# A graph convolution with a two-expert feed-forward layer: the order of the prelude, and where the first node tile's counts, its sums and one check stand

## The chip, the cores and the metric

The kernel runs on one core of a Trainium2 chip. The core has five engines, each with its own instruction queue worked off in order: PE (TensorE, matmuls; PEld are its weight loads), DVE (VectorE), ACT (ScalarE), POOL (GpSimd) and SP (SyncE, which here only issues DMAs). They wait for each other through semaphores. The metric is the device time of one execution in microseconds (us). Three runs of the kernel before gave 1189.58, 1190.65 and 1191.01 us; the median is 1190.65.

## The reference

6250 nodes with 256 features and 206250 edges (100000 drawn ones in both directions, and one loop per node), sorted by destination. First a graph convolution with a residual, then a feed-forward layer of eight experts with a residual, of which the two best of one common routing are used for all nodes:

```python
deg = segment_sum(ones, dst) + 1                  # a second loop per node is added
dinv = rsqrt(deg)
h = layernorm(x) @ W
out = segment_sum(h[src] * (dinv[src] * dinv[dst])[:, None], dst) + b
x = x + where(out > 0, out, prelu_a * out)
...
y = einsum(gelu(einsum(x, W1) + b1), W2) + b2     # per expert
x = x + layernorm(sum of the top-2 experts' y * weight + x) * gamma + beta
```

## The kernel before

Nodes are cut into 49 tiles of 128 (`NT`). For the first 41 node tiles (`NDT`) the neighbour sums are dense: a matrix of edge counts of one destination tile against all 49 source tiles is built from one-hot vectors (`one_hots` on DVE, `counts` on PE, a copy `a_t` by ACT in `counts`), and is multiplied with the scaled h (`sums` on PE, 49 matmuls of 128x512 per node tile; h is held in two parts, high and low, side by side, hence 512). For the last 8 tiles (`NGT`) rows of h are gathered by indirect DMA and summed by one-hot matmuls (`g_hot`, `g_sums`, `fetch`).

Everything up to that is the prelude, and the change is there. Its order is written out by hand: inside `manual_schedule` every engine gets its instructions in program order, so the order of the calls is the order of each queue.

- `x_load(i)` (L223) loads seven node tiles of x by SP. `h_step(m)` (L354) transposes two node tiles of x on PE (`pt`, L361), copies them by ACT (`xT`, L365), multiplies the pair of the step before with the centred weight on PE (`p`, L372) and copies that to `hk` by ACT (L376). There are 26 steps; `h_some(n)` (L380) runs the next n. `p` has two buffers (`ps_h`).
- `x_stats(i)` (L389) takes the statistics of seven node tiles on DVE (L391); from them `rs`, 1/sqrt of the variance, is made (L515 to L523).
- `search(w)` (L406) finds, on ACT and DVE, where the edges of 5 node groups begin (w = 0 to 4), and POOL gathers their packed edges from memory (`run`, L427, five indirect DMAs; three buffers). `keys(w)` (L437, DVE) makes keys of them, `turn_keys(w)` (L445) transposes keys and low parts on PE and copies them by ACT to `keyT` and `loT` (L457), `key_hots(w)` (L462, DVE) derives from `keyT` what the degrees are counted from (`ev`).
- Then the degrees: 49 thin matmuls (L529), `deg` on DVE (L535), a square root on ACT (L536), its reciprocal on DVE (L545), and `sc` = `rs` x `dinv` (L546).
- `least` is the least key, for a check of the edge list; `less` (L538 to L544) halves `keyT` by minima down to 400 elements before the reduction at L554. `pto`, `tto` (L548 to L552) are sums over the degrees from which `g_at` (L582) is made, the place of the gathered tiles' edges.
- `parts(n)` (L558) scales node tile n of h by `sc`: the high part on ACT (L565), the low one on DVE (L571), or, for every fifth tile after the first 14, on ACT and POOL (L568, L569).
- The main part (from L587) opens with the remaining `parts`, in between which the counts of tile 0 are placed (L798 to L808). `keep(i)` (L785) writes seven finished node tiles to memory by SP, for the gathers. `g_edges()` (L701) gathers on POOL the edges of the last 8 tiles.
- The loop (L812) handles node tile n in four quarters: one-hots of the next tile, counts of tile n + 1 (L817), a quarter of the sums of n (L819), and the tile before is finished (`node`, `stat`). `own(n)` adds the extra loop of each node. After tile `G0` - 2 = 2 `g_check()` (L709) puts the checks together, with a matmul on PE in its middle (L724); the result decides later on whether a slow fallback runs.

Buffers that matter: `hk` is in two halves (`h_room(0)`, `h_room(1)`, 24 node tiles each, `HK` = 24) that lie where the count matrices of even and odd tiles come later (tags a0 and a1), so counts of tile 0 can be stored only when the parts of tiles 0 to 23 have been read. `one_hots` has two pairs of buffers, the count results in PSUM (`pa`) four.

Of the kernel before, what the change touches and what calls it, by code (L numbers as in the profile page):

```python
# [11 lines left out]
F32 = mybir.dt.float32  # L12
BF16 = mybir.dt.bfloat16
# [21 lines left out]
def gnn_moe_kernel(  # L35
# [147 lines left out]
    with ExitStack() as ph:  # L183
# [196 lines left out]
        def h_some(n):  # L380

            for m in itertools.islice(steps, n):
                h_step(m)
                n -= 1
            return n == 0
# [3 lines left out]
        def x_stats(i):  # L389
            for t in range(TB):  # L390
                nc.vector.bn_stats(st[:, i * TB + t, :], xbs[i][:, t, :])  # L391
# [79 lines left out]
        for i in range(2, NB_T):  # L471
            x_load(i)
        for _ in range(3):
            h_some(2)
            search(_)
            if _ > 0:
                x_stats(_ - 1)
        h_some(2)
        search(3)
        keys(0)  # L480
        h_room(1)
        hk.append((2 * HK, 1, hk2))
        h_some(1)
        turn_keys(0)
        x_stats(2)
        h_some(1)
        key_hots(0)
        search(4)
        h_some(1)
        keys(1)  # L490
        h_some(1)
        turn_keys(1)
        x_stats(3)
        h_some(1)
        key_hots(1)
        h_some(1)
        keys(2)
        turn_keys(2)
        x_stats(4)
        h_some(1)  # L500
        key_hots(2)
        h_some(2)
        keys(3)
        turn_keys(3)
        x_stats(5)
        h_some(1)
        key_hots(3)
        h_some(2)
        keys(4)
        turn_keys(4)  # L510
        x_stats(6)

        dm = ep.tile([P, NT], F32, name="dm")
        va = ep.tile([P, NT], F32, name="va")
        nc.vector.tensor_tensor(dm, st[:, :, 1], st[:, :, 4], OP.subtract)  # L515
        nc.vector.tensor_tensor(va, st[:, :, 2], st[:, :, 5], OP.add)
        nc.vector.scalar_tensor_tensor(dm, dm, 0.25, dm, op0=OP.mult, op1=OP.mult)
        nc.vector.scalar_tensor_tensor(va, va, 1.0 / D, dm, op0=OP.mult, op1=OP.add)
        nc.vector.tensor_scalar(va, va, LN_EPS, None, op0=OP.add)
        nc.scalar.activation(rs, va, AF.Sqrt)  # L520
        h_some(1)
        key_hots(4)
        nc.vector.reciprocal(rs, rs)  # L523
        h_some(1)

# [10 lines left out]
        nc.scalar.activation(dinv, deg, AF.Sqrt)  # L536
        nc.vector.tensor_reduce(tot[:, 0:1], deg, AX.X, OP.add)
        less = rp_.tile([P, WP, P, 2], F32, name="run")  # L538
        less = less.rearrange("p j e f -> p (j e f)").bitcast(BF16)
        halves, m = keyT, NPR  # L540
        while m > 400:
            m //= 2
            nc.vector.tensor_tensor(less[:, :m], halves[:, :m], halves[:, m : 2 * m], OP.min)
            halves = less  # L544
        nc.vector.reciprocal(dinv, dinv)  # L545
        nc.vector.tensor_tensor(sc, rs, dinv, OP.mult)  # L546

        pto = ps_h.tile([P, 2, D], F32, name="p")  # L548
        nc.tensor.matmul(pto[:NT, 0, :P], deg, ones, start=True, stop=True)
        tto = ep.tile([P, P], F32, name="tto")  # L550
        nc.scalar.copy(tto[:NT], pto[:NT, 0, :P])
        nc.tensor.matmul(pto[:, 1, :NGT], tto[:NT], g_before[:NT], start=True, stop=True)  # L552
        least = ep.tile([P, 1], F32, name="least")
        nc.vector.tensor_reduce(least, less[:, :m], AX.X, OP.min)  # L554
        nc.vector.tensor_scalar(tot[:, 1:2], least, 0.0, None, op0=OP.is_lt)


# [18 lines left out]
        while h_some(1):  # L576
            for n in itertools.islice(ns, 2):
                parts(n)
        g_s = ep.tile([P, NGT], F32, name="g_s")
        nc.vector.tensor_tensor(g_s, pto[:, 1, :NGT], g_first, OP.subtract)  # L580
        nc.vector.tensor_scalar(g_s, g_s, 0.0, float(E - GE), op0=OP.max, op1=OP.min)
        nc.vector.tensor_scalar(g_at, g_s, g_part, None, op0=OP.add)  # L582
        nc.vector.tensor_reduce(tot[:, 3:4], deg[:, NDT:], AX.X, OP.add)
        for n in itertools.islice(ns, 4):
            parts(n)

    with main:  # L587
# [121 lines left out]
        def g_check():  # L709
# [3 lines left out]
                op0=OP.mult, op1=OP.add,  # L713
            )
            some = gp.tile([P, 2 * D], F32R, name="rows").bitcast(F32)[:, : NGT * GC]
            flat = g_neg.rearrange("p g c -> p (g c)")
# [73 lines left out]

        kept = 0
        for n in ns:
            parts(n)
            if n % TB == TB - 1:
                for kept in range(kept, n // TB + 1):
                    keep(kept)
                kept += 1
            if n == HK - 6:  # L798
                one_hots(0)
                one_hots(1)  # L800
            if n in (HK + 6, NT - 1):
                c = 0 if n < NT - 1 else 2
                for b in range(NBH):
                    counts(0, c * NBH + b)
                one_hots(c + 2)
                for b in range(NBH):
                    counts(0, (c + 1) * NBH + b)
                one_hots(c + 3) if c == 0 else None  # L808
        g_edges()

        assert NHG == QT
        for n in range(NDT):  # L812
            for c in range(NHG):
# [456 lines left out]
```

## Time and profile before

The page describes one execution of 1190.92 us; the span from its first to its last instruction is 1189.1 us. The mean granted clock of TensorE was 0.962.

| engine | busy us | share of the span |
|---|---|---|
| PE | 1100.9 | 93% |
| PEld | 842.6 | 71% |
| DVE | 711.5 | 60% |
| ACT | 630.9 | 53% |
| POOL | 529.1 | 44% |

The share is a mean over stages. By windows of the timeline, with the busy us of each engine in it:

| stretch, us | PE | DVE | ACT | POOL | granted clock |
|---|---|---|---|---|---|
| 0 to 20 | 11.95 | 14.03 | 3.85 | 7.99 | 1.00 |
| 20 to 40 | 14.32 | 10.81 | 12.63 | 10.97 | 0.93 |
| 40 to 60 | 19.05 | 16.91 | 13.75 | 15.55 | 0.89 |
| 60 to 80 | 18.17 | 13.63 | 12.52 | 0.95 | 0.96 |
| 80 to 100 | 9.62 | 12.71 | 15.44 | 4.02 | 0.76 |
| 100 to 120 | 6.11 | 20.00 | 16.56 | 10.35 | 0.50 |
| 120 to 140 | 20.00 | 11.33 | 8.49 | 15.73 | 0.93 |
| 140 to 160 | 20.00 | 16.13 | 9.68 | 4.38 | 1.00 |

The first four rows are the edges, the steps of h and the keys; the degrees are at 75 to 80 us, the parts from 82 to 117, and the loop over node tiles runs from about 119 to 790 us. Behind it come the routing and the feed-forward stage, up to 1189. The granted clock is the share of TensorE's full speed that the throttle gave; at 0.50 a matmul takes about twice as long. In lines of the timeline the columns are: start, duration, engine, line, operation, what is written and read, the shapes, how often, and in brackets the idle time of the engine before it with what ended it.

### The profile page before, as it was taken

To read this page: it belongs to the slowest core of one execution; us is meant where nothing else is said; L and a number is where in the kernel's file an instruction comes from. 1 tells how busy PE (TensorE), PEld (TensorE's weight loads), DVE (VectorE), ACT (ScalarE), POOL (GpSimd) and SP (SyncE) were. 2 spreads that over 40 slices of the span, in tenths; PEclk is the share of its full clock that TensorE was granted. 3 is DMA by queue.
4 is the path that set the end of the run, shared out by engine and by line. 5 is a ranking of instruction groups with operands and counts; after the bars stand their busy time and mean duration, and the time that the engine had idled before them with its cause. 6 is when DMAs were issued, how large, how long until landed. Compare 5 with 4: busy or idle time off the path is not lost. (4 is left out here: it accounts for less than half of the span.)

```text
span 1189.1 us, 18227 instructions
## 1 busy us (share of the span) xinstructions
PE 1100.9 (93%) x6706; PEld 842.6 (71%) x6706; DVE 711.5 (60%) x1509; ACT 630.9 (53%) x1547; POOL 529.1 (44%) x526
## 2 busy tenths in 40 slices
PE   7882999999999999999999999952999999999996
PEld 5671878888888888888888888841666666666665
DVE  6759677788787887878878788653222232222222
ACT  3658446666666666666666666611333333333332
POOL 3704703555565555655556555400333333334433
PEclk9895999999999999999999999985999999999998
DMA  8708603565655656556565565504011111111000
GB/s 266 227 12 323 187 27 98 143 155 147 153 141 143 156 146 154 138 143 157 146 154 138 144 157 144 133 23 135 14 42 49 37 36 36 36 36 36 23 18 22
DMA packets 92254, 133.11 MB, mean 112 GB/s; under 512 B 8830, under 2 KB 47390, under 8 KB 92158
## 3 DMA queue, kind: packets, MB, share of 16 engines
q0 software_dynamic: 43584, 80.40, 27.6%
q1 hardware_dynamic: 45266, 49.06, 12.6%
q10 hardware_dynamic: 3308, 2.41, 0.7%
q8 instruction: 54, 0.88, 0.3%
q14 instruction: 42, 0.34, 0.1%
HBM read 104.47 MB, written 27.37 MB: 111 GB/s over the span
## 5 line engine op out<-in xcount | busy, mean ns | idle before, releaser
L659 PE MATMUL po<-hp,a_t 128*128 128x512 f32 x2009 | 504.2, 400 | 0.0
L745 POOL DMA_INDIRECT rows<-hl_d,g_src x288 | 329.2, 1143 | 299.1 <-PE pg L776 228.5
L659 PEld LDWEIGHTS po<-hp,a_t 128*128 128x128 f32 x2009 | 367.1, 189 | 72.7
L643 ACT CAST a_t<-pa 128x392 fp32r<-128x392 f32 x656 | 271.0, 501 | 206.2 <-PE pa L639 204.5
L605 DVE TENSOR_TENSOR oh_lo<-iota,loT 128x2048 bf16<-128x2048 bf16 x164 | 199.5, 1216 | 15.9 <-PE pa L639 15.9
L639 PEld LDWEIGHTS <-oh_lo 128*128 128x128 bf16 x2624 | 128.5, 99 | 68.2 <-issue 25.4
L1200 PE MATMUL p<-xT,w_sb 128*128 128x512 f32 (+1 forms) x416 | 172.6, 573 | 2.5 <-ACT hT L1204 1.8
L639 PE MATMUL pa<-oh_key,oh_lo 128*128 128x98 bf16 x2624 | 153.6, 211 | 22.9 <-DVE oh_key L605 12.3
L1218 PE MATMUL p<-w_sb,hT 128*128 128x256 f32 (+1 forms) x784 | 172.9, 381 | 0.0
L1218 PEld LDWEIGHTS p<-w_sb,hT 128*128 128x128 f32 (+1 forms) x784 | 148.5, 191 | 20.2
L605 DVE TENSOR_TENSOR oh_key<-iota,keyT 128x1568 bf16<-128x1568 bf16 x164 | 158.2, 965 | 0.0
L1200 PEld LDWEIGHTS p<-xT,w_sb 128*128 128x128 f32 x416 | 77.6, 192 | 90.9 <-issue 86.4
L1223 DVE TENSOR_TENSOR yt<-yt,p 128x256 f32<-128x256 f32 (+1 forms) x49 | 20.6, 421 | 164.3 <-PE p L1218 164.3
L1184 POOL TENSOR_TENSOR yt<-yt,b_sb 128x1024 f32<-128x1024 f32 (+1 forms) x13 | 29.1, 2242 | 184.0 <-PE px L1178 124.6
L1204 ACT ACTIVATE hT<-p,b_sb 128x512 f32<-128x512 f32 (+1 forms) x104 | 67.5, 661 | 79.0 <-PE p L1200 78.7
L759 ACT ACTIVATE oh_g<-iota_f,g_dst 128x128 fp32r<-128x128 f32 x288 | 103.8, 425 | 0.0
L776 PE MATMUL pg<-rows,oh_g 128*128 128x512 f32 x288 | 91.1, 397 | 0.0
L1228 ACT ACTIVATE rs<-rs 128x1 f32<-128x1 f32 (+1 forms) x49 | 9.9, 203 | 146.4 <-DVE rs L1227 146.4
L674 DVE TENSOR_TENSOR x<-x,po 128x256 f32<-128x256 f32 x41 | 17.3, 422 | 104.9 <-ACT x L673 104.9
L1233 POOL TENSOR_TENSOR yt<-yt,gamma_bc 128x256 f32<-128x256 f32 (+1 forms) x49 | 35.5, 725 | 90.2 <-DVE yt L1230 90.2
L760 ACT ACTIVATE oh_g<-oh_g 128x256 fp32r<-128x256 f32 x144 | 60.3, 419 | 4.5
L1173 DVE TENSOR_SCALAR yt<-xt,mean,rstd 128x256 f32<-128x256 f32 x49 | 18.8, 444 | 73.0 <-DMA xt<-x_d 72.8
(195 smaller groups left out, 863.3 us busy)
## 6 DMA issues: line engine op xcount, KB each, us to landing
hl_d<-hp SPq DMA_DIRECT2D x7, 1792.0 KB, 10.9
x_d<-x SPq DMA_DIRECT2D x49, 128.0 KB, 1.7
xt<-x_d SPq DMA_DIRECT2D x12, 512.0 KB, 3.9
out_dram<-yt SPq DMA_DIRECT2D x48, 128.0 KB, 1.7
xb<-in_x_dram SPq DMA_DIRECT2D x6, 896.0 KB, 11.9
xs<-in_x_dram SPq DMA_DIRECT2D x41, 128.0 KB, 3.4
rows<-hl_d,g_src POOLq DMA_INDIRECT x288, 3.8
w_sb<-in_L_ffn_W_dram ACTq DMA_DIRECT2D x2, 512.0 KB, 7.8
```

The costliest lines, as they stand in the source:

```text
L605: nc.vector.tensor_tensor(oh, iota2[:, :m, :].unsqueeze(1).to_broadcast([P, HG // 2, m, 2]), v[:, s].rearrange("p (q t) -> p q t", t=2).un ...
L639: nc.tensor.matmul(pa[:, i].rearrange("p j h -> p (j h)"), oh_lo[:, q, :, t], oh_key[:, q, :, t], start=True, stop=True,)
L643: nc.scalar.copy(tiles[n][:, :, b * 2 * BG : (b + 1) * 2 * BG], pa.rearrange("p i j h -> p h (i j)"),)
L659: nc.tensor.matmul(pouts[n].rearrange("p k d -> p (k d)"), tiles[n][:, g, :], hp2[g // TB][:, g % TB].rearrange("p k d -> p (k d)"), start ...
L745: nc.gpsimd.indirect_dma_start(out=g_rows[j], out_offset=None, in_=hl_d, in_offset=bass.IndirectOffsetOnAxis(ap=g_src[:, j // GC, j % GC : ...
L759: nc.scalar.activation(oh[:, i, :], iota_f, AF.Abs, bias=g_neg[:, g, c : c + 1])
L760: nc.scalar.activation(oh, oh.bitcast(F32), AF.Relu, scale=-1.0, bias=1.0)
L776: nc.tensor.matmul(pouts[n].rearrange("p k d -> p (k d)"), oh[:, i, :], g_rows.pop(j0 + i), start=False, stop=((j0 + i) % GC == GC - 1),)
L1200: nc.tensor.matmul(p1[:, :cols], w1_sb[:, e, k, f * P : (f + 1) * P], xT[:, k, :cols], start=(k == 0), stop=(k == ND - 1),)
L1204: nc.scalar.activation(hT[:, e, f, :cols], p1[:, :cols], AF.Gelu, bias=b1_sb[:, e, f : f + 1])
L1218: nc.tensor.matmul(p2[:r], hT[:, e, f, t * P : t * P + r], w2_sb[:, e, f, :], start=(e == 0 and f == 0), stop=(e == TOP_K - 1 and f == NF ...
L1233: nc.gpsimd.tensor_tensor(y, y, gamma_bc[:r], OP.mult)
```

## The change

The h steps are spread in another way: twelve of the 26 come ahead of the first `keys`, then two or three between one turn of keys and its hots, one in the last round, and none between the last hots and the degrees; three are left for the loop with the parts. The statistics follow the keys by three batches. `search(4)` comes ahead of the first keys. The halvings of `less` go; the least key is taken by one reduction over all 3200 elements of `keyT`, in `g_check`. `pto`, `tto` and the sum of the degrees come behind the last steps of h. The first one-hots of tile 0 come directly behind the prelude, its counts at parts 23, 27 and 31, its sums from part 32 on, each behind the part that it uses; the one-hots of tile 1 begin at parts 38 and 44, its counts follow the last part. The loop then begins at tile 1.

```diff
@@ -470,58 +470,40 @@
 
         for i in range(2, NB_T):
             x_load(i)
-        for _ in range(3):
-            h_some(2)
-            search(_)
-            if _ > 0:
-                x_stats(_ - 1)
+        h_some(2)
+        search(0)
+        h_some(2)
+        search(1)
+        x_stats(0)
+        h_some(2)
+        search(2)
+        x_stats(1)
         h_some(2)
         search(3)
-        keys(0)
+        h_some(1)
+        search(4)
+        x_stats(2)
         h_room(1)
         hk.append((2 * HK, 1, hk2))
-        h_some(1)
-        turn_keys(0)
-        x_stats(2)
-        h_some(1)
-        key_hots(0)
-        search(4)
-        h_some(1)
-        keys(1)
-        h_some(1)
-        turn_keys(1)
-        x_stats(3)
-        h_some(1)
-        key_hots(1)
-        h_some(1)
-        keys(2)
-        turn_keys(2)
-        x_stats(4)
-        h_some(1)
-        key_hots(2)
-        h_some(2)
-        keys(3)
-        turn_keys(3)
-        x_stats(5)
-        h_some(1)
-        key_hots(3)
-        h_some(2)
-        keys(4)
-        turn_keys(4)
-        x_stats(6)
+        h_some(3)
 
         dm = ep.tile([P, NT], F32, name="dm")
         va = ep.tile([P, NT], F32, name="va")
-        nc.vector.tensor_tensor(dm, st[:, :, 1], st[:, :, 4], OP.subtract)
-        nc.vector.tensor_tensor(va, st[:, :, 2], st[:, :, 5], OP.add)
-        nc.vector.scalar_tensor_tensor(dm, dm, 0.25, dm, op0=OP.mult, op1=OP.mult)
-        nc.vector.scalar_tensor_tensor(va, va, 1.0 / D, dm, op0=OP.mult, op1=OP.add)
-        nc.vector.tensor_scalar(va, va, LN_EPS, None, op0=OP.add)
-        nc.scalar.activation(rs, va, AF.Sqrt)
-        h_some(1)
-        key_hots(4)
+        for w in range(NW):
+            keys(w)
+            turn_keys(w)
+            if w + 3 < NB_T:
+                x_stats(w + 3)
+            if w + 4 == NB_T:
+                nc.vector.tensor_tensor(dm, st[:, :, 1], st[:, :, 4], OP.subtract)
+                nc.vector.tensor_tensor(va, st[:, :, 2], st[:, :, 5], OP.add)
+                nc.vector.scalar_tensor_tensor(dm, dm, 0.25, dm, op0=OP.mult, op1=OP.mult)
+                nc.vector.scalar_tensor_tensor(va, va, 1.0 / D, dm, op0=OP.mult, op1=OP.add)
+                nc.vector.tensor_scalar(va, va, LN_EPS, None, op0=OP.add)
+                nc.scalar.activation(rs, va, AF.Sqrt)
+            h_some(1 if w == NW - 1 else 2 + w % 2)
+            key_hots(w)
         nc.vector.reciprocal(rs, rs)
-        h_some(1)
 
 
         pdeg = pcnt[:, NW : NW + NT]
@@ -534,26 +516,8 @@
         deg = ep.tile([P, NT], F32, name="deg")
         nc.vector.tensor_scalar(deg, pdeg, 1.0, None, op0=OP.add)
         nc.scalar.activation(dinv, deg, AF.Sqrt)
-        nc.vector.tensor_reduce(tot[:, 0:1], deg, AX.X, OP.add)
-        less = rp_.tile([P, WP, P, 2], F32, name="run")
-        less = less.rearrange("p j e f -> p (j e f)").bitcast(BF16)
-        halves, m = keyT, NPR
-        while m > 400:
-            m //= 2
-            nc.vector.tensor_tensor(less[:, :m], halves[:, :m], halves[:, m : 2 * m], OP.min)
-            halves = less
         nc.vector.reciprocal(dinv, dinv)
         nc.vector.tensor_tensor(sc, rs, dinv, OP.mult)
-
-        pto = ps_h.tile([P, 2, D], F32, name="p")
-        nc.tensor.matmul(pto[:NT, 0, :P], deg, ones, start=True, stop=True)
-        tto = ep.tile([P, P], F32, name="tto")
-        nc.scalar.copy(tto[:NT], pto[:NT, 0, :P])
-        nc.tensor.matmul(pto[:, 1, :NGT], tto[:NT], g_before[:NT], start=True, stop=True)
-        least = ep.tile([P, 1], F32, name="least")
-        nc.vector.tensor_reduce(least, less[:, :m], AX.X, OP.min)
-        nc.vector.tensor_scalar(tot[:, 1:2], least, 0.0, None, op0=OP.is_lt)
-
 
         def parts(n):
             i, t = divmod(n, TB)
@@ -576,13 +540,18 @@
         while h_some(1):
             for n in itertools.islice(ns, 2):
                 parts(n)
+
+        pto = ps_h.tile([P, 2, D], F32, name="p")
+        nc.tensor.matmul(pto[:NT, 0, :P], deg, ones, start=True, stop=True)
+        tto = ep.tile([P, P], F32, name="tto")
+        nc.scalar.copy(tto[:NT], pto[:NT, 0, :P])
+        nc.tensor.matmul(pto[:, 1, :NGT], tto[:NT], g_before[:NT], start=True, stop=True)
         g_s = ep.tile([P, NGT], F32, name="g_s")
         nc.vector.tensor_tensor(g_s, pto[:, 1, :NGT], g_first, OP.subtract)
         nc.vector.tensor_scalar(g_s, g_s, 0.0, float(E - GE), op0=OP.max, op1=OP.min)
         nc.vector.tensor_scalar(g_at, g_s, g_part, None, op0=OP.add)
         nc.vector.tensor_reduce(tot[:, 3:4], deg[:, NDT:], AX.X, OP.add)
-        for n in itertools.islice(ns, 4):
-            parts(n)
+        nc.vector.tensor_reduce(tot[:, 0:1], deg, AX.X, OP.add)
 
     with main:
         b_bc = bcast_row(wide, gnn_b, "b_bc", nc.sync)
@@ -712,6 +681,9 @@
                 g_neg, g_dst, -1.0, g_first.unsqueeze(2).to_broadcast([P, NGT, GC]),
                 op0=OP.mult, op1=OP.add,
             )
+            least = np_.tile([P, 1], F32, name="least", bufs=1)
+            nc.vector.tensor_reduce(least, keyT, AX.X, OP.min)
+            nc.vector.tensor_scalar(tot[:, 1:2], least, 0.0, None, op0=OP.is_lt)
             some = gp.tile([P, 2 * D], F32R, name="rows").bitcast(F32)[:, : NGT * GC]
             flat = g_neg.rearrange("p g c -> p (g c)")
             nc.vector.tensor_scalar(some, flat, 0.5, None, op0=OP.is_lt)
@@ -789,27 +761,37 @@
             )
 
         kept = 0
+        one_hots(0)
         for n in ns:
             parts(n)
             if n % TB == TB - 1:
                 for kept in range(kept, n // TB + 1):
                     keep(kept)
                 kept += 1
-            if n == HK - 6:
-                one_hots(0)
+            if n == HK // 2:
                 one_hots(1)
-            if n in (HK + 6, NT - 1):
-                c = 0 if n < NT - 1 else 2
-                for b in range(NBH):
-                    counts(0, c * NBH + b)
-                one_hots(c + 2)
-                for b in range(NBH):
-                    counts(0, (c + 1) * NBH + b)
-                one_hots(c + 3) if c == 0 else None
+            if n in (HK - 1, HK + 3, HK + 7):
+                for c in range(2) if n == HK - 1 else (2 + n // (HK + 7),):
+                    for b in range(NBH):
+                        counts(0, c * NBH + b)
+                if n < HK + 7:
+                    one_hots(2 + n // (HK + 3))
+            if n > HK + 7:
+
+                sums(0, 0 if n == HK + 8 else n - 1, n)
+            if n in (HK + 14, NT - 5):
+                one_hots(NHG + (n != HK + 14))
+        own(0)
+        for c in range(NHG):
+            for b in range(NBH):
+                counts(1, c * NBH + b)
+            one_hots(NHG + 2 + c) if c < 3 else None
+            if c == 0:
+                sums(0, NT - 1, NT)
         g_edges()
 
         assert NHG == QT
-        for n in range(NDT):
+        for n in range(1, NDT):
             for c in range(NHG):
                 q = (n - G0) * NHG + c
                 g_hot(q * GQ)
```

## What the change should do to the time

> **What bounds the kernel now.** First the 40 slices of the span, about 29.7 us each. PE reads 9 in nearly every slice from the sixth on; the first five slices are not full, and all edits but one lie in them (the other one, in `g_check`, falls into the sixth).
>
> ```profile
> PE   7882999999999999999999999952999999999996
> PEclk9895999999999999999999999985999999999998
> ```
>
> The chain of waits doesn't reach these slices: it begins at 815.7 us, after the branch of the fallback, and shows only PE's matmuls of the last stage. So I read the timeline up to 180 us, and then windows. From 130 us on PE is busy without a gap up to about 750 us, but for one place at 164 us. What the change does to the time is therefore read at two clocks: when PE begins tile 1 of the main loop (the matmuls of `counts(2, 0)`, 135.02 us), and how long PE stands still at 164 us. The rest is PE's own work and is left as it is.
>
> The timeline of the degrees. Columns: start, duration, what, idle before it.
>
> ```profile
> 73.65 1.99 PE L372 MATMUL p<-w_sb,xT 128*128 128x256 f32 x8 [1.08 <-ACT xT L365]
> ...
> 75.26 1.49 PEld L529 LDWEIGHTS <-ev 128*128 128x128 bf16 x49
> ...
> 76.88 0.21 DVE L535 TENSOR_SCALAR deg<-pcnt 128x49 f32<-128x49 f32 x1 [3.26 <-PE pcnt L529]
> 77.12 0.25 ACT L536 ACTIVATE dinv<-deg 128x49 f32<-128x49 f32 x1 [0.86 <-DVE deg L535]
> ...
> 79.15 0.46 DVE L545 RECIPROCAL dinv<-dinv 128x49 f32<-128x49 f32 x1
> 79.64 0.21 DVE L546 TENSOR_TENSOR sc<-rs,dinv 128x49 f32<-128x49 f32 x1
> ```
>
> See that the square root is done at 77.37 and its reciprocal starts at 79.15: the halvings of `less` stand before it in DVE's queue. Every `parts(n)` needs `sc`.
>
> Windows of 4 us in the stretch of the parts. Columns: length, then busy us of PE, PEld, DVE, ACT, POOL, then the granted clock.
>
> ```profile
> 34.00:38.00 4.00, 1.14 (x6) 0.66 (x4) 0.32 (x2) 2.14 (x6) 2.93 (x4) 0.92 1.07 347
> ...
> 98.00:102.00 4.00, 1.49 (x16) 1.36 (x17) 4.00 (x6) 3.19 (x8) 4.00 (x3) 0.50 1.03 385
> 102.00:106.00 4.00, 1.65 (x16) 1.31 (x15) 4.00 (x8) 2.70 (x8) 0.54 (x1) 0.50 1.03 373
> 106.00:110.00 4.00, 1.49 (x16) 1.38 (x17) 4.00 (x5) 4.00 (x12) 1.26 (x1) 0.50 1.02 377
> 110.00:114.00 4.00, 0.00 (x0) 0.00 (x0) 4.00 (x10) 4.00 (x12) 1.62 (x2) 0.50 1.04 385
> ```
>
> DVE is full, PE nearly empty and at half clock. Tile 0's 49 sums come only behind this stretch (119.9 to 135.0 us).
>
> The timeline of the check:
>
> ```profile
> 165.14 0.45 DVE L721 TENSOR_REDUCE tot<-rows 128x1 f32<-128x288 f32 x1
> 165.63 0.16 DVE L722 TENSOR_TENSOR tot<-tot 128x1 f32<-128x1 f32 x1
> ...
> 165.85 0.38 PE L724 MATMUL pg<-tot,ones 128*128 128x3 f32 x2 [1.57 <-DVE tot L722]
> ...
> 166.80 4.18 PEld L659 LDWEIGHTS po<-hp,a_t 128*128 128x128 f32 x12
> 166.82 4.59 PE L659 MATMUL po<-hp,a_t 128*128 128x512 f32 x12
> ```
>
> PE's previous sums end at 164.28, DVE enters the check at 163.82: DVE is only 0.46 us ahead, so what is added there is PE's wait.
>
> **1. Steps of h, keys, degrees.** Until 35.13 us the order is the same: PE has nine steps behind it. A step takes 2.16 us (transposes at 62.73 and 64.90), a turn of keys 0.56 (62.17 to 62.73). Before, 13 more steps and 5 turns are 28.1 + 2.8 = 30.9, plus PE's idle 4.66 us for the first keys (35.13 to 39.79; DVE waited for the gather), 2.15 for the half clock after it (39.79 to 44.66 took 4.87 instead of 2.72), 0.95 for `search(4)` and 1.08 for the table of the square root: 74.9 against a measured 75.26. After, 14 more steps and 5 turns are 33.0. The steps ahead of the first keys cover the gather, so 4.66 and 2.15 go. `search(4)`'s 2.5 us of ACT stand in front of two steps' copies: 1.5 us in place of 0.95. The table costs 1.0 as before. PE is free at 35.13 + 33.0 + 2.5 = 70.7. Late next are the last keys: from turn to hots measured 3.76 us (69.23 to 72.99), with one step beside it, turn at 68.0, hots done 71.7. PE waits 1.0; degrees at 71.7 rather than 75.26, **3.5 us earlier**, with one step fewer left behind them. What hides the rest: x tile 21 is wanted at 39.5 us, its load landed 14 us after issue at worst (before 37); the last keys' gathers are issued by POOL until 61.1 us, paced by 1.25 us each in both orders, and land within 2.7 to 6.0 us, for a use at 65.1 (at worst 1 us late). `search(4)`'s five gathers move up in the order, but stand in POOL's queue behind those of `search(3)`, whose buffer is given free by `turn_keys(0)` at 43.7, before POOL arrives (47.5). The steps of h issue no DMA.
>
> **2. Degrees to `sc`.** Without halvings the reciprocal follows the root: 77.42 + 0.46 + 0.24 = 78.12 instead of 79.85, **1.7 us**. `sc` stands at 71.7 + 2.86 = 74.6 against 79.85.
>
> **3. The last steps.** Three remain, on two free buffers of `p`, since `pto` comes after them: PE's waits on ACT's `hk` (0.24, 0.46, 0.68) go. Played forward with ACT's rows (copies 0.57, scalings 0.41), six parts and `pto`'s chain end at 81.6, where `one_hots(0)` can start. Unknown is the clock: before, the thin matmuls of the degrees and the gaps behind them brought it to half from about 78.3 to 81.8 (windows of 1 us read 0.67, 0.50, 0.50, 0.62), and one step took 4.1 us instead of its 2.16 or so. Now the thin stretch is 2.5 us long instead of 2.8, with no `pto` in it: between 0 and 2.3 us on the way through ACT's copies. I take 1.2, the middle: the row speaks for the half clock, the shorter stretch against it. DVE starts the one-hots at **82.8**, ACT is free at 81.2.
>
> **4. Parts with tile 0 beside them.** A part takes ACT 0.41, DVE 0.42 (0.56 beside POOL's), a pair of one-hots 2.02 (96.11 to 98.12), eight casts 3.3. DVE: `one_hots(0)`, parts to 12, `one_hots(1)`, parts to 23: 94.3. The casts of tile 0 go into the buffer that holds h of nodes below 24, so ACT, through at 89.0, waits for DVE's part 23 (before: 1.55 us at 103.30): 5.2 us lost on ACT. Then 8 casts to 97.6, parts 24 to 27, 4 casts, parts 28 to 31, last cast at 105.0. DVE ends part 48 at 117.0, just as before (116.6): the early one-hots of tile 1 fill it. But PE now begins tile 0's sums at 105.5: some eight at half clock (0.43; the first twelve before took 4.27 in all), 40 at 0.25, done at 118.7. Then counts of tile 1 (0.92), three pairs of one-hots in a row on DVE, each behind counts (3 x 2.02), and the loop starts at 118.7 + 0.92 + 6.1 = **125.7**. The same bookkeeping on the order before gives 135.9 for the measured 135.02. PE has gaps of up to 1 us in this last stretch; if it enters the loop at half clock that costs 1.7: I take half, 0.8. So 126.5: **8.5 us gained**; from both ends 5 to 11.
>
> SP's queue: the loads `xs` waited for DVE's L583 and move up with it; the seven `keep` follow the parts, and the last leaves at 117 as before. POOL: `g_edges` stands behind part 44, at about 113 us (before 114.47), its 16 gathers end near 138; the check wants them at 156.
>
> **5. The check.** Reductions: 0.204 for 49 elements (L537), 0.562 for 400 bf16 (L554), so 1.02 ns each; 3200 give 0.562 + 2800 x 1.02 = 3.42, with the comparison and gaps **3.65**, all on PE's wait (5.2 instead of 1.57). The Trainium skill speaks against it (VectorE: DVE Perf Modes, Rules for kernel authors: a reduction on the hot path runs at 1x, the slowest of DVE's operations, restructure). The removed halvings are such a restructuring: 0.98 + 0.94 + 0.56 = 2.5 us by their rows, so by the rule's form the check would cost 2.7 instead of 3.65. The single reduction is what runs; 3.65 stands.
>
> The clock: TensorE: Matmul & The Clock Gate (HAM oscillation) says that gaps of PE up to about 3.4 us leave it at full clock. The row says otherwise: after 1.57 us of gap the clock was 0.54 at 167 and 0.50 until 170, and twelve sums took 4.59 instead of 3.01. By the rule the half clock would be new (+1.6); by the row it is paid already, and the longer gap can add up to one more us or save one. I go by the row: **+0.4**, 3.2 to 5.5 for the whole check.
>
> **Sum.** Profiled execution 1190.92 (span 1189.1 plus 1.8 around it; the median is 0.27 lower). 1190.92 - 8.5 + 3.65 + 0.4 = **1186.5 us**, own range 1183 to 1190. Less than 0.2% (2.4 us: below 1188.3, above 1193.0) can't be told from no change.
>
> **Rivals.**
> - Half clock throughout (slower). If tile 0's sums, fed by one part at a time, never give PE a full stretch, 48 x 0.43 = 20.6 puts their end at 125.7 and the loop at 133.4, with 2 us of half clock in it: gain -0.4, check 4.05: **1195**. For it: clock 0.50 from 92 to 122 us. Against: 32 sums are ready at once, and 3.7 us of dense work sufficed at 118.7. It decides from some 35 sums at half clock. Chance 0.13.
> - The gains are eaten on the way: half clock behind the degrees, late keys, ACT's wait at part 23 longer; loop at about 130: **1190**. Chance 0.20.
> - The check's reduction is hidden, because DVE comes to it some 4 us ahead of PE: **1182.4**. Against: DVE's 0.46 us of lead. Chance 0.12.
> - Forecast: 0.55.
>
> Faster: 0.48 of the forecast, the third, a little of the second: 0.64; same 0.20; slower 0.16. Range 1181.5 to 1191.5: it leaves out the first rival and a little of the third.
>
> **What would show it.** The first weights of the degree matmuls near 71.7; `sc` near 74.6; PE busy from 105 to 118 with the clock back at 1 from about 109; `counts(2, 0)` near 126; a new TENSOR_REDUCE of 3.4 us and a wait of PE near 5.2. I am wrong if PE waits for the run gathers between 43 and 70, if the casts end well after 105, or if a second place in the loop shows PE idle.

## The result, and the profile after

| kernel | median us | runs from to | ratio to before, 95% |
|---|---|---|---|
| before | 1189.83 (6 runs) | 1186.91 to 1191.01 | |
| changed | 1183.85 (6 runs) | 1180.11 to 1187.75 | 0.9957 [0.9942, 0.9971] |

The changed kernel is faster by 0.43%, some 5.1 us by the ratio and 6.0 by the medians. Its profiled execution took 1185.34 us (span 1183.6, mean granted clock 0.966), against 1190.92 (1189.1, 0.962). Line numbers below are those of the kernel that the row belongs to; in the changed one the degree matmuls are L511, `sc` L520, the low parts L535, counts L608, sums L628, the check's matmul L696. The experiments below were run in three sets on two chips, and on one of them the kernel before itself takes 1210 us; so each ratio is to the kernel before in the same set, and the last experiments come back to that chip. Which chip the comparison above ran on is not on record.

The 40 slices of the changed kernel, 29.6 us each:

```profile
PE   6975989999999999999999999952999999999996
PEclk9987889999999999999999999985999999999999
```

PE's third to fifth slices read 7, 5, 9 where they read 8, 2, 9: the nearly empty stretch of the parts is no longer empty. The sixth, which holds the check, reads 8 where it read 9; behind it nothing has changed to the eye.

The timeline of the degrees, changed kernel (start, duration, what, idle before it):

```profile
72.74 1.38 PE L511 MATMUL pcnt<-ones_b,ev 128*128 128x1 bf16 x49 [0.92 <-DVE ev L467]
...
74.40 0.25 ACT L518 ACTIVATE dinv<-deg 128x49 f32<-128x49 f32 x1 [1.96 <-DVE deg L517]
...
74.68 0.47 DVE L519 RECIPROCAL dinv<-dinv 128x49 f32<-128x49 f32 x1 [0.31 <-ACT dinv L518]
...
75.18 0.21 DVE L520 TENSOR_TENSOR sc<-rs,dinv 128x49 f32<-128x49 f32 x1
```

The degrees begin at 72.74 (their first matmul was at 75.48), the reciprocal follows the root directly, and `sc` stands at 75.39 instead of 79.85. The one wait that remains ahead of the degrees is for the last keys' hots, 0.92 us.

The entry of the loop in the kernel before, PE (tile 1's first counts, sums, and the next quarter's counts):

```profile
135.02 0.92 PE L639 MATMUL pa<-oh_key,oh_lo 128*128 128x98 bf16 x16
135.76 3.00 PE L659 MATMUL po<-hp,a_t 128*128 128x512 f32 x12
138.60 0.91 PE L639 MATMUL pa<-oh_key,oh_lo 128*128 128x98 bf16 x16
```

The timeline of tile 0 and of the entry of the loop, ACT and PE of the changed kernel:

```profile
95.22 3.21 ACT L612 CAST a_t<-pa 128x392 fp32r<-128x392 f32 x8 [5.02 <-DVE hp L535]
...
105.52 12.97 PE L628 MATMUL po<-hp,a_t 128*128 128x512 f32 x48 [0.86 <-ACT a_t L612]
...
121.45 0.92 PE L608 MATMUL pa<-oh_key,oh_lo 128*128 128x98 bf16 x16 [0.68 <-DVE oh_key L574]
123.47 1.49 PE L608 MATMUL pa<-oh_key,oh_lo 128*128 128x98 bf16 x16 [1.10 <-DVE oh_key L574]
125.49 1.49 PE L608 MATMUL pa<-oh_key,oh_lo 128*128 128x98 bf16 x16 [0.53 <-DVE oh_key L574]
126.76 4.40 PE L628 MATMUL po<-hp,a_t 128*128 128x512 f32 x12
131.00 0.93 PE L608 MATMUL pa<-oh_key,oh_lo 128*128 128x98 bf16 x16
```

ACT stands 5.02 us until DVE has read the last of the first 24 tiles; 48 sums run beside the parts at 0.27 us each; tile 1 of the loop (`counts(2, 0)`) begins at 125.49 where it began at 135.02. See also the two counts that took 1.49 instead of 0.92, and the twelve sums that took 4.40 instead of 3.00: PE enters the loop at half clock, so the next quarter begins 5.51 us later rather than 3.58, and of 9.53 us gained 7.60 are left at that point (131.00 against 138.60).

The timeline of the check, changed kernel:

```profile
156.62 3.48 DVE L685 TENSOR_REDUCE least<-keyT 128x1 f32<-128x3200 bf16 x1
...
161.74 0.58 PE L696 MATMUL pg<-tot,ones 128*128 128x3 f32 x2 [5.04 <-DVE tot L694]
...
162.18 1.47 PE L608 MATMUL pa<-oh_key,oh_lo 128*128 128x98 bf16 x16
...
163.44 4.79 PE L628 MATMUL po<-hp,a_t 128*128 128x512 f32 x12
...
168.07 0.91 PE L608 MATMUL pa<-oh_key,oh_lo 128*128 128x98 bf16 x16
```

PE waits 5.04 us instead of 1.57. The quarter after the check begins at 168.07, against 171.26 before:

```profile
171.26 0.93 PE L639 MATMUL pa<-oh_key,oh_lo 128*128 128x98 bf16 x16
```

So of the 7.60 us, 3.19 are left. The remainder of the difference between the spans (5.5 us) comes in two pieces behind it. The first, 0.96 us, grows evenly over the loop up to the last sums, by about 13 ns in every two quarters. It goes with the halvings: from the quarter after the check to the last sums all seven profiles of kernels that have them take 605.09 to 605.11 us, and the five of kernels without them and with the check in its old place take 604.14 or 604.15. Why is open. The second, 1.34 us, is at the very end, where the last 14 matmuls of the feed-forward stage took 4.51 us in the profile of before, most of them at half clock, and 3.19 here. That is chance: four of all 14 profiles (before, the reduction twice, the reduction in DVE's gaps, the halvings back again) have 4.51 to 4.72 there and the other ten 3.19.

### The profile page after: what moved, and what is told of

Read it like the earlier page. It is cut to its first block, busy times and chain, and to the rows that moved or that the text cites. A ratio compares the mean times of both kernels' runs of the same rounds, so it can differ in the third digit from the quotient of the medians.

```text
span 1183.6 us, 18224 instructions
## 1 busy us (share of the span) xinstructions
PE 1100.2 (93%) x6706; PEld 846.2 (71%) x6706; DVE 712.4 (60%) x1506; ACT 630.0 (53%) x1547; POOL 526.8 (45%) x526
## 5 line engine op out<-in xcount | busy, mean ns | idle before, releaser
L628 PE MATMUL po<-hp,a_t 128*128 128x512 f32 x2009 | 505.8, 402 | 0.9 <-ACT a_t L612 0.9
L628 PEld LDWEIGHTS po<-hp,a_t 128*128 128x128 f32 x2009 | 369.5, 190 | 73.2 <-ACT a_t L612 1.1
L608 PEld LDWEIGHTS <-oh_lo 128*128 128x128 bf16 x2624 | 130.9, 100 | 60.1 <-issue 20.3
L608 PE MATMUL pa<-oh_key,oh_lo 128*128 128x98 bf16 x2624 | 156.5, 212 | 17.8 <-ACT a_t L612 8.3
L748 PEld LDWEIGHTS pg<-rows,oh_g 128*128 128x128 f32 x288 | 54.7, 190 | 11.9
```

The costliest lines, as they stand in the source:

```text
L608: nc.tensor.matmul(pa[:, i].rearrange("p j h -> p (j h)"), oh_lo[:, q, :, t], oh_key[:, q, :, t], start=True, stop=True,)
L628: nc.tensor.matmul(pouts[n].rearrange("p k d -> p (k d)"), tiles[n][:, g, :], hp2[g // TB][:, g % TB].rearrange("p k d -> p (k d)"), start ...
L748: nc.tensor.matmul(pouts[n].rearrange("p k d -> p (k d)"), oh[:, i, :], g_rows.pop(j0 + i), start=False, stop=((j0 + i) % GC == GC - 1),)
```

## The experiments

The theory was the prediction's: tile 0's sums beside the parts and the earlier `sc` gain some 8.5 us at the entry of the loop, and the check gives about 4 back. Its rivals were that one part alone makes the gain, that the sums gain nothing, and that the check's length costs clock as well as the wait.

### The halvings back in their place

```diff
+        (halvings of less)          # ahead of reciprocal(dinv), as before
         nc.vector.reciprocal(dinv, dinv)
         nc.vector.tensor_tensor(sc, rs, dinv, OP.mult)
+        (least from less)
...
-            nc.vector.tensor_reduce(least, keyT, AX.X, OP.min)   # in g_check
```

> The changed kernel, but the least key is taken by the old halvings ahead of the reciprocal of the degrees, and the check has no reduction of its own. Marks of the changed kernel: sc at 75.4 us, tile 1 of the loop at 125.5, PE's wait in the check 5.04. Theory (the halvings cost on the way to sc, the one reduction costs in the check, each on the path): sc about 1.75 us later (77.1), tile 1 near 127.2, wait in the check back to 1.6; in sum about 1.8 us less than the changed kernel. Rival (DVE has room in the check, the wait there comes from something else): the wait stays near 5, and the kernel is 1.7 us slower than the changed one.

Its timeline at the degrees, DVE:

```profile
98.20 0.21 DVE L517 TENSOR_SCALAR deg<-pcnt 128x49 f32<-128x49 f32 x1 [1.21 <-PE pcnt L511]
98.33 0.98 DVE L524 TENSOR_TENSOR run<-keyT 128x1600 bf16<-128x1600 bf16 x1
99.35 0.97 DVE L524 TENSOR_TENSOR run<-run 128x800 bf16<-128x800 bf16 x2
100.24 0.46 DVE L526 RECIPROCAL dinv<-dinv 128x49 f32<-128x49 f32 x1
```

The reciprocal waits behind the halvings again; from the first degree matmul to the end of `sc` it is 4.15 us instead of 2.65, so the halvings cost 1.5 us on the path. PE's wait in the check is 1.58. That much is as expected. The time is not: 1213.35 (ratio 1.0021 [1.0002, 1.0040]) on a chip on which the kernel before took 1210.83, and the degrees come at 96.79 where the changed kernel has them at 72.74. What happens there is taken up below.

### The check's reduction twice

```diff
+            for _ in range(2):
-            nc.vector.tensor_reduce(least, keyT, AX.X, OP.min)
+                nc.vector.tensor_reduce(least, keyT, AX.X, OP.min)
```

> The changed kernel with the 3200-element reduction in the check done twice. Theory (all of it stands on PE's wait): the wait in the check 5.04 + 3.5 = 8.5 us, and the place in the loop after it later by just that, since the clock is at half after the pause in either case. Rival (the length of the pause decides the clock): up to 1.7 us more on top. Second rival (hidden): wait unchanged.

Timeline of the check in this kernel, PE:

```profile
193.97 0.59 PE L697 MATMUL pg<-tot,ones 128*128 128x3 f32 x2 [8.54 <-DVE tot L695]
194.42 1.47 PE L608 MATMUL pa<-oh_key,oh_lo 128*128 128x98 bf16 x16
195.67 4.14 PE L628 MATMUL po<-hp,a_t 128*128 128x512 f32 x12
199.65 0.91 PE L608 MATMUL pa<-oh_key,oh_lo 128*128 128x98 bf16 x16
```

The wait is 8.54 against 5.04: the second reduction lies on PE's wait to its full 3.5 us, and the half clock behind it does not last longer for that (5.23 us from the counts to the next quarter, 5.89 with one reduction). One run on the same chip as above gave 1218.43; the marks carry this reading, not the time.

### The order of the steps alone

The kernel before with nothing but the new order of steps, searches, keys and statistics; halvings, `pto` and everything from the parts on as before.

> The kernel before with the new order of the h steps, keys and statistics alone; halvings, pto, counts, sums and check as before. Before: degrees' first weights at 75.26, sc at 79.85, tile 1 at 135.02. Theory: degrees near 72.7 as in the changed kernel, sc near 77.1, three steps instead of four behind it; tile 1 near 130.4, 4.6 us less in all (ratio 0.996). Rival (the gain comes from the counts and sums of tile 0, the order only shifts work): tile 1 at 133 or later, under 2 us.

1215.89, ratio 1.0036 [1.0021, 1.0050]: slower by about 4.4 us where 4.6 less was expected, with the degrees at 95.68. The theory fails on this chip, and its rival, a gain under 2 us, did not foresee a loss either.

### Tile 0 early alone

The kernel before up to the degrees, halvings and `pto` included, and the changed one from the parts on, without its reduction in the check.

> The kernel before up to the degrees (halvings and pto included), with only the counts of tile 0 early and its sums following the parts. Theory: one-hots of tile 0 start near 91.9, eight parts done, so tile 1 of the loop near 132.6, a gain of 2.4 us at its start, of which the half clock at the entry takes 1.9: about 0.5 us in all, not to be told from none. Rival (this part brings most of the change): tile 1 near 128 and 5 us less.

1202.62, ratio 0.9960 [0.9936, 0.9984]: faster by about 4.8 us, the rival's size and not the 0.5 expected. Its degrees come at 84.97, some 11 us ahead of those of the new order on the same chip. Tile 1 begins at 143.78 and, entered at half clock, takes 6.18 us to the next quarter; how much earlier than before that is can't be said, since the kernel before was not profiled on this chip.

### The sums behind the parts

Tile 0's counts stay early; only the sums go, in one block, behind the first counts of tile 1.

```diff
-            if n > HK + 7:
-                sums(0, 0 if n == HK + 8 else n - 1, n)
...
-                sums(0, NT - 1, NT)
+                sums(0, 0, NT)
```

> The changed kernel, but the 49 sums of tile 0 are done in one go behind the last part and the first counts of tile 1. Theory (their place beside the parts hides about 10 us of them): tile 1 near 135 instead of 125.5, entered at full clock (its first quarter 3.6 us instead of 5.5), about 7.6 us more in all. Rival (the chain of one-hots and casts of tile 1 sets the start of the loop, not the sums): tile 1 before 128.

Timeline of PE (other chip, kernel before 1189.26):

```profile
110.18 1.49 PE L608 MATMUL pa<-oh_key,oh_lo 128*128 128x98 bf16 x16 [6.76 <-ACT hp L529]
111.45 13.00 PE L628 MATMUL po<-hp,a_t 128*128 128x512 f32 x49
...
129.43 0.92 PE L608 MATMUL pa<-oh_key,oh_lo 128*128 128x98 bf16 x16 [1.08 <-DVE oh_key L574]
130.16 2.99 PE L628 MATMUL po<-hp,a_t 128*128 128x512 f32 x12
133.00 0.91 PE L608 MATMUL pa<-oh_key,oh_lo 128*128 128x98 bf16 x16
```

It did not serve quite as meant. The one-hots of tile 1 are ready early, so its counts start at 110.18 and the block still runs beside the last parts, from 111.45. Measured from the first one-hots of tile 0 (82.58 here, 83.82 in the changed kernel), tile 1 begins 5.2 us later than in the changed kernel. But PE has two gaps ahead of it instead of three, behind a dense block, and enters at full clock (3.57 us to the next quarter), so only 3.24 us are left of that. The one run gave 1187.24. This one profile says two things: moving the block loses some 5 us and not the 9.5 expected, since much of it still runs beside the last parts; and the thin entry that the changed kernel pays costs about 1.9. What the sums would cost with no part beside them was not run.

### The reduction in DVE's gaps

The least key in two pieces where DVE has nothing else to do for PE: 2000 elements after part 23, 1200 after `own(0)`; in the check only the comparison is left.

```diff
                     one_hots(2 + n // (HK + 3))
+                if n == HK - 1:
+                    nc.vector.tensor_reduce(least[:, 0:1], keyT[:, :2000], AX.X, OP.min)
...
         own(0)
+        nc.vector.tensor_reduce(least[:, 1:2], keyT[:, 2000:], AX.X, OP.min)
+        nc.vector.tensor_tensor(least[:, 2:3], least[:, 0:1], least[:, 1:2], OP.min)
```

> The changed kernel with the reduction taken in two pieces where DVE stands idle: 2000 elements behind the one-hots of part 23 (idle of 2.49 us there) and 1200 behind own(0) (idle of 1.57). Theory: tile 1 at 125.5 to 126, wait in the check 1.6 to 1.8 instead of 5.04, 3.3 us less than the changed kernel. Rival (no true gaps, the pieces push the parts and one-hots back): tile 1 up to 3.6 later, no gain.

1180.63, ratio 0.9912 [0.9888, 0.9936], below the changed kernel's interval. The pieces took 2.22 and 1.40 us, and tile 1 begins at 125.29, not later than the 125.49 of the changed kernel: the gaps did hide them. Timeline of the check, PE:

```profile
158.07 0.38 PE L694 MATMUL pg<-tot,ones 128*128 128x3 f32 x2 [1.57 <-DVE tot L692]
158.32 0.91 PE L608 MATMUL pa<-oh_key,oh_lo 128*128 128x98 bf16 x16
159.05 3.00 PE L628 MATMUL po<-hp,a_t 128*128 128x512 f32 x12
161.89 0.91 PE L608 MATMUL pa<-oh_key,oh_lo 128*128 128x98 bf16 x16
```

The wait is the old 1.57, but what follows it runs at full clock, 3.57 us to the next quarter. The quarter after the check begins 6.18 us ahead of that of the changed kernel. So the reduction in the check cost more than its own length: 3.47 us of wait, and 2.5 us of clock and of the matmul itself against this execution, in which the pause of 1.57 left the clock alone.

### The check's matmul later, and a filled entry

The first kernel adds to the last one that the check's matmul and what depends on it are issued two quarters of a tile later, by when DVE is done (`g_bad`). The second adds twelve matmuls to that, four behind each of the counts of tile 1 that PE waits around; their results are read by nobody.

```diff
+                if n == G0 - 1 and c == 1:
+                    g_bad()
...
             if c == 0:
                 sums(0, NT - 1, NT)
+            else:
+                fill(4)             # 4 matmuls of 128x512
```

> As the run with the reduction in gaps, and the check's matmul with what follows it is issued two quarters of a tile later than its DVE part. Theory (a pause of 1.6 us is enough to halve the clock, as the row of before has it): PE's wait of 1.6 to 1.8 and the half clock behind it, another 1.8, both go: 3.5 us less than with the reduction in gaps alone. Rival (pauses [...]leave the clock alone): only the wait goes, 1.7 us. Second rival (DVE then is late with the next one-hots): nothing gained.

> As the run with the check's matmul later, and 12 filler matmuls of 128x512, whose result nobody reads, in PE's gaps between the counts of tile 1. Theory (the half clock at the entry of the loop comes from these gaps): the loop's first quarter takes 3.6 us instead of 5.5, 1.9 us less. Rival (the fillers push the counts back, or the gaps are not what halves the clock): no gain, up to 1 us more.

1175.60, ratio 0.9888 [0.9869, 0.9906], and 1173.60, ratio 0.9868 [0.9848, 0.9888]. The first has no wait of PE at the check any more, and still enters the loop at half clock (123.54 to 128.69, 5.15 us). In the profiles only about 1.6 us of its gain over the two-piece reduction stand at the check, as the rival had it: the pause there had left the clock alone. Another 1.6 stand ahead of the first one-hots, where the clock stayed at 1.00 behind the degrees, and 1.35 in the last 14 matmuls; both are chance. Timeline of PE at the entry with the fillers (L675):

```profile
119.09 1.18 PE L675 MATMUL pg<-hp,ident_r 128*128 128x512 f32 x4
120.11 0.93 PE L608 MATMUL pa<-oh_key,oh_lo 128*128 128x98 bf16 x16
120.85 1.17 PE L675 MATMUL pg<-hp,ident_r 128*128 128x512 f32 x4
...
123.99 0.92 PE L608 MATMUL pa<-oh_key,oh_lo 128*128 128x98 bf16 x16
124.73 2.99 PE L628 MATMUL po<-hp,a_t 128*128 128x512 f32 x12
127.56 0.91 PE L608 MATMUL pa<-oh_key,oh_lo 128*128 128x98 bf16 x16
```

Every matmul is at full clock and the quarter takes 3.57 us. Measured from the first one-hots of tile 0 the next quarter is 45.19 us off, against 46.71: the fillers bring 1.5 us where PE had nothing else to do. In time it is 2.0 us by the medians, and this last kernel takes about 15.7 us less than the one before.

### The chip with 1210 us

The first four experiments ran on one chip, the next four on another. Three of the first four kernels and the changed kernel itself were put once more on the first chip.

> The changed kernel itself, beside the parts of it below. Theory: about 5 us less than before (ratio 0.996), degrees' first matmul near 72.7, tile 1 near 125.5. Rival: where the loads of code are slow (pauses of PE and ACT in the prelude that the profile names issue or remote, as in the first four runs), the new order loses some 10 us on the way to the degrees, and the kernel is no faster than before.

> The same kernel as the order of the steps alone, measured again because PE and ACT paused for some 20 us in the prelude of that execution with nothing in the profile to name. Theory as there: degrees near 72.7, sc near 77.1, tile 1 near 130.4, 4.6 us less than before. Rival: tile 1 at 133 or later, under 2 us.

> The same kernel as tile 0 early alone, again. Theory as there: tile 1 near 132.6, the half clock at the entry takes 1.9 of the 2.4 us, so about 0.5 us in all. Rival: tile 1 near 128, 5 us less.

> The same kernel as the halvings put back, again. Theory: sc 1.75 us later than in the changed kernel, the check's wait 1.6 instead of 5.04, about 1.8 us less than the changed kernel in all.

| kernel, that chip | first time | again |
|---|---|---|
| before | 1210.83 us | 1210.44 us |
| changed | | 1.0039 [1.0012, 1.0066] |
| order of the steps alone | 1.0036 [1.0021, 1.0050] | 1.0044 [1.0030, 1.0059] |
| tile 0 early alone | 0.9960 [0.9936, 0.9984] | 0.9961 [0.9942, 0.9980] |
| changed, halvings back | 1.0021 [1.0002, 1.0040] | 1.0005 [0.9987, 1.0022] |

So it repeats: on this chip the changed kernel is slower than the one before by some 4.7 us, tile 0 early alone gains as much, and the order of the steps alone loses it. The three parts about add up there: -4.7 for tile 0, +4.4 to +5.3 for the order, +4.1 for the least key in the check (1.0039 less 1.0005). The intervals are some 2 to 3 us to either side, the first measurement of the halvings would make the last term 2.2, and the move of `pto` is in no kernel alone.

Where the order loses can be seen in windows of 4 us (length, busy us of PE, PEld, DVE, ACT, POOL with counts, granted clock, share of the DMA engines, GB/s). First the changed kernel on that chip:

```profile
38.00:42.00 4.00, 0.58 (x1) 0.50 (x2) 1.75 (x6) 0.61 (x2) 3.08 (x4) 0.84 1.08 349
...
46.00:50.00 4.00, 0.05 (x1) 0.00 (x0) 0.00 (x0) 0.04 (x1) 0.95 (x1) 0.50 0.34 98
```

and then the changed kernel in the first comparison:

```profile
38.00:42.00 4.00, 3.07 (x19) 2.50 (x18) 2.81 (x9) 2.86 (x8) 3.01 (x4) 1.00 1.10 358
...
46.00:50.00 4.00, 4.00 (x31) 3.57 (x30) 3.97 (x9) 2.70 (x6) 3.09 (x4) 1.00 0.45 122
```

Where one has PE and DVE full, in the other PE, DVE and ACT stand. The execution that was profiled took 1226.07 us, 8.9 more than the median of its runs, so its pieces are not those of a typical one. The timeline of ACT and POOL in it:

```profile
49.96 0.59 ACT L376 COPY hk<-p 128x512 f32<-128x512 f32 x1 [8.59 <-remote]
...
60.57 0.95 POOL L427 DMA_INDIRECT run<-pk_d,r_i  x1 [13.41 <-PE pk L455]
```

ACT stands 8.59 us. The product that it copies was done at 45.2, so for the last 4.8 it waits for something that no record shows ("remote"). Such a stop is in the profile of every kernel on that chip and ends there between 47 and 50 us; no profile of the other runs has it. The two orders differ in what follows it. In the old order (tile 0 early alone, again) `turn_keys(0)` has run before the stop, at 40.5, so a buffer of `run` is free and POOL goes on with its gathers at 50.3; it waits 2.85 and 3.18 us in all. In the new order `turn_keys(0)` stands behind the twelfth step, at 59.58, POOL stands for 13.41 us, and its last gathers leave at 60.6 to 73.1. Among them comes a second stop, of PE (2.11 us, nothing shown that it waits for) and of ACT:

```profile
67.20 0.60 PE L361 MATMUL pt<-ident_r,xb 128*128 128x128 f32 x4
69.91 1.99 PE L372 MATMUL p<-w_sb,xT 128*128 128x256 f32 x8 [2.11 <-issue]
71.74 0.60 PE L361 MATMUL pt<-ident_r,xb 128*128 128x128 f32 x4
75.64 3.78 PE L372 MATMUL p<-w_sb,xT 128*128 128x256 f32 x8 [3.30 <-ACT xT L365]
```

These are PE's lines in the timeline of the same execution: two steps that take 4.3 us undisturbed begin at 67.2 and end at 79.2, the second one at half clock. From ACT's return to the degrees the new order needs 47.6 us and the old one 35.1; of the 12.5 between them some 7.7 are this second stop, 2.2 one more step ahead of the degrees, and 2.6 are not accounted for. PE's part of it (2.0 to 2.1 us) is in all six profiles of the new order on that chip and in neither of the old order's; so are POOL's long wait (10.5 to 14.2 us against 3.2 at most) and the late degrees (93.0 to 97.5 against 85.0).

I had put the stops down to code that is loaded late while the DMA engines are full (share 1.08). The trace doesn't carry that: no packet of the instruction queues lands between 19 and 51 us in that execution, and the next one starts at 51.2, when ACT has been running for 1.2 us. What the engines wait for is open. So is whether the late gathers bring the second stop on or only lie beside it, and where the kernel before loses its 20 us there, since it was not profiled on that chip.

The prelude is not the only place where that chip loses. At the entry of the loop PE's counts of tile 1 come in fours, with a wait ahead of nearly every four, for a cast or for nothing shown (the same execution, two of them):

```profile
151.53 0.49 PE L608 MATMUL pa<-oh_key,oh_lo 128*128 128x98 bf16 x4 [1.82 <-issue]
155.16 0.49 PE L608 MATMUL pa<-oh_key,oh_lo 128*128 128x98 bf16 x4 [1.70 <-ACT a_t L612]
```

From the first one-hots of tile 0 to the loop's second quarter the changed kernel takes 62.4 us here, where it took 47.2 in the first comparison. The other five profiles with tile 0 early on that chip have 48.7 to 59.5, and one kernel, with the halvings back, has 50.4 and 59.5. The order alone has 45.6 and 51.2, where the kernel before had 42.5 in its one profile. So up to 15 us of one execution's time there are lost behind the prelude; what causes them is open too, and so is which part of the change, if any, brings them on.

## Why the prediction was right

**The degrees (step 1).** Predicted 71.7, measured 72.74; 2.5 us earlier than the first weights of before (75.26) instead of 3.5. The first keys are turned at 43.68 (43.7 predicted), and PE's wait for the last hots is 0.92 for 1.0. The missing 1.0 is PE's own work: its tenth step begins at 35.54, 0.4 behind the 35.13 that I had counted from, and fourteen steps and five turns take 34.1 us (35.54 to 71.82, less its waits) where I had 33.0; the waits among them are 2.2 for 2.5. Most of the 1.1 is in the three steps with a wait: 2.61, 3.37 and 3.49 us with waits of 0.18, 0.93 and 1.07, so that each takes about 0.26 more than the 2.17 of a step and its wait. So the last keys are turned at 68.93 and not at 68.0.

**`sc` (step 2).** Predicted 74.6, measured 75.39: the delay of step 1, less 0.2. The halvings were priced at 1.7; taken back they cost 1.5.

**The last steps (step 3).** One-hots at 82.8 predicted, 83.82 measured, the same delay plus 0.2. The half clock behind the degrees came, so the 1.2 us in the middle of its bounds was near. But it was one outcome of two: from `sc` to the first one-hots 8.37 to 8.43 us pass in four profiles of this order (changed, changed again, reduction twice, two-piece reduction), and 6.74 or 6.75 in three (sums behind the parts, check's matmul later, fillers), where the clock is at 1.00 throughout.

**Parts with tile 0 (step 4).** First sums at 105.5 predicted, 105.52 measured; ACT's wait 5.2 and 5.02; DVE's last part 117.0 and 117.5; tile 1 at 125.7 and 125.49. Most of the delay of 1 us was still there when DVE ended part 23 (95.1 for 94.3), half of it at the last cast (105.5 for 105.0), and none at the first sum; what lay between was priced a little high. The rival of half clock throughout is gone: 48 sums took 12.97 us, 0.27 each, not 0.43.

The half clock on entry was taken at half of its price, 0.8; it cost 1.93. So 7.6 us were gained and not 8.5. The sums behind the parts and the fillers show that this is the price of the gaps: with two of them behind a dense block, or with all of them filled, the same quarter took 3.57.

**The check (step 5).** Reduction 3.48 for 3.42, PE's wait 5.04 for 5.2: as priced, and the doubled reduction puts its whole length on PE. Whether the restructured form (halvings) would cost less inside the check was not run; on the way to `sc` it cost 1.5. The clock is the term that was mis-sized: +0.4 predicted, +0.92 measured with the check's matmul (161.74 to 168.07, against 165.85 to 171.26), and against a check that leaves the clock alone, as in the two-piece reduction, 2.5. I had taken the half clock after the old pause as a fixed property of that row. It was one outcome of two (last section). The rule that I set aside held in five of the eight profiles with the short pause, and in all four with a longer one half clock came, as it says.

**Sum.** Predicted 1186.5 for an execution like the profiled one, 1185.34 measured. By steps: 9.5 - 1.9 - 4.4 = 3.2 us at the check instead of 4.45, then 0.96 over the loop, which comes with the change and which I had not foreseen, and 1.34 in the last 14 matmuls, which is chance. Without the chance the sum would be near 1186.8: two misses all but cancel, 1.3 us of gain too much at the entry and the check, and 1.0 over the loop that was not foreseen. The half clock behind the check in the profile of before was chance as well; with the other outcome that execution would have been 1.6 us shorter. The direction rests on the steps of the change; the closeness of the figure is in part luck.

**What I had not seen.** I judged the order of the steps by one chip's profile, and said of POOL only that `turn_keys(0)` frees its buffer in time. That held there, with 3.8 us to spare (43.7 against 47.5). On the other chip, where the engines stop, POOL loses over 10 us to this one dependence, and the whole change loses time; that the one brings the other is not shown. How much the order alone brings where nothing stops wasn't timed; the marks say 2.5 us at the degrees.

## What to carry to other kernels

A reduction that is moved off one path is not free in another: look for the stretch where the engine is idle and cut it to fit there, as the two-piece reduction did for 5.4 us (0.9957 against 0.9912). A wait of PE should be priced with the clock behind it: where half clock came, it cost 1.6 to 2.6 us per pause here. And a thin entry into a dense loop can be filled with matmuls that nobody reads. An order that holds a buffer longer should be judged on more than one chip, with an eye to what the engine behind it loses in a stop.

## What the runs showed of the hardware

**A pause of 1.57 us halves the clock or doesn't.** Eight profiles have a pause of 1.57 or 1.58 us at the check. From the counts behind it to the next quarter three took 5.14 to 5.17 us (before; the halvings back, first time; the order alone, again) and five 3.57 or 3.58. All three with 5.03 or 5.04 took 5.89 to 6.21, the one with 8.54 took 5.23. That fits the Trainium skill (TensorE: Matmul & The Clock Gate, What's actually happening), which says that the window over which activity is judged runs freely, so that the same kernel finds it in different phases; its limit of some 3.4 us for gaps (HAM oscillation) is not a safe one, as three of eight show.

**Several short gaps do it too.** The gaps of 0.5 to 1.2 us between counts at the entry of the loop left PE at half clock in the profiles of four kernels (changed, tile 0 early alone, two-piece reduction, check's matmul later: 5.15 to 6.18 us for a quarter). With two of them behind a dense block (sums behind the parts), or with fillers in them, it was 3.57.

**One chip stops where another doesn't.** The stops of 7 to 11 us on ACT in the prelude were in all eight profiles from the one chip and in none of the six others, the changed kernel being among both, and the entry of the loop was slower there as well (48.7 to 62.4 us to its second quarter with tile 0 early, against 45.2 to 50.4); a comparison made on one chip can change its sign on another.
